# Last stage of a graph network with experts: per-partition layout, a sum on TensorE, and batches of unequal size

## The chip, the cores and the metric

The kernel runs on one core of a Trainium2 chip. A core has five engines that work side by side: TensorE (PE; its weight loads are shown apart as PEld), VectorE (DVE), ScalarE (ACT), GpSimd (POOL) and SyncE (SP), which here issues most of the transfers. Each engine works through its own list of instructions in order and waits on semaphores for the others. Sixteen DMA engines move data between the chip's memory (DRAM) and the on-chip memory SBUF; TensorE writes its results to another memory, PSUM, of eight banks, and each bank holds 512 numbers of four bytes in each partition.

The metric is the time on the device in microseconds (us), the median of several runs. A profile is one further execution, recorded instruction by instruction.

## The reference

Two layers are computed over 6250 nodes of 256 numbers each. The first gathers the 100,000 edges of each node and runs a small network over them. The second, which matters here, sends each node to two of 16 experts:

```
logits  = xn @ gate_w + gate_b                # xn: the normalised node
top 2 experts per node, weights w by softmax of their logits
moe     = sum over the two of  w_k * ((relu(xn @ w1[e_k] + b1[e_k])) @ w2[e_k] + b2[e_k])
y       = xn + moe
out     = x1 + (y - mean(y)) / sqrt(var(y) + 1e-5) * gamma + beta
```

Here x1 is the node after the first layer. All numbers have four bytes.

## The kernel before, in words

Nodes are taken in 50 tiles (NT) of P = 125, one node in each partition. The program has three stages that bear on the change.

**The graph stage** ends by writing x1 to DRAM (x1_d) and by sorting each node, twice, into the rows of its two experts (xg_d).

**The expert stage** works through blocks of 256 sorted rows, at most 57 of them here (NS). For a block, load_block (L996) fetches rows, weights and bias on SP's queue, three blocks ahead. run_block (L1025) multiplies with the first weights in two halves (L1034), and turn_block (L1007) in between transposes the next block: four transposes on TensorE, a copy on VectorE (xT, L1014), the addition of xb and eb (L1017), and two small operations that make the addresses. The first half's activation is ScalarE's (L1040), the second half's is VectorE's (hb, L1038). Then come the second weights (L1047), the addition of the block's input on VectorE (L1050), the scaling by w on ScalarE (L1052), and two scatters from GpSimd (L1053), which put each row back in the order of the nodes: the first choice of node n to row n of y_d, the second to row N + n. The input xn is part of what is scattered, in shares that add up to it, so that y is the sum of the two rows.

**The filling of X** is done during the expert stage. X1 in SBUF holds x1 for all 50 tiles. load_x1 (L979) is called after every third block from block 15 on; it adds beta to the five tiles that the call before has loaded (L984, one VectorE operation of 125x1280) and issues the loads of the next five. Since the order of each engine's list is the order of the program text (manual_schedule), that addition stands on VectorE between L1050 of one block and L1014 for the next one.

**The last stage** (L1353 to L1400) waits for the last scatter. It takes ten batches of five tiles (FS). In each: two loads from y_d, one for each choice, each split in partitions 0 to 79 and 80 to 124 (halves, L100); the addition of the two (L1365); for each tile, statistics in two operations (L1370, L1371); a root on ScalarE (L1372) and a reciprocal and a bias on VectorE (L1377, L1378); the normalisation of each tile on ScalarE (L1382); the product with gamma and the addition of X (L1386, L1387); and the stores. The products of a batch are written between the statistics and the reciprocal of the next one. A node lies in partition p of tile i as row i * 125 + p ("(i p) d -> p i d"), so each partition takes five separate rows of 1 KB from DRAM for a batch. Three batches are loaded ahead, in four pairs of buffers.

Of the kernel before, what the change touches and what calls it, by code (L numbers as in the profile page):

```python
# [9 lines left out]
F32 = mybir.dt.float32  # L10
# [3 lines left out]
AF = mybir.ActivationFunctionType  # L14
OP = mybir.AluOpType
AX = mybir.AxisListType
PSUM = bass.MemoryType.PSUM
DRAM = bass.MemoryType.DRAM

P = 125  # L20
PA = 80
RR = 8
GW = 2
WE = 20
JR = (6, 5, 5, 10, 21, 20, 28)
GR = (1, 1, 1, 2, 3, 2, 1)
JS = 3
KB = 250
GS = 4
FS = 5  # L30
SB = 256
NA = 14
NS = 57
SLOTS = 12
SLOT = 4.6
IB = (1, 1, 1, 2, 3, 5)
# [5 lines left out]
def kernel(  # L42
# [18 lines left out]
    nc = tc.nc  # L61
    N, D = x.shape
    E, EF = edge.shape
# [3 lines left out]
    NT = N // P  # L67
    EJ = E // P
# [12 lines left out]
    NG = (NT + GS - 1) // GS  # L81
    ER = EP * sum(JR)
# [1 line left out]
    REG = [(ER - EP * sum(JR[:c + 1]), j) for c, j in enumerate(JR)]  # L84
    N0 = NT - GS * (NG - 1)
    GRP = [(GS * (NG - 1 - g), GS * (NG - 1 - g) + (GS if g else N0)) for g in range(NG)]
    assert N == NT * P and E == EJ * P and ER % (E // 100) == 0 and NT % FS == 0 and GW + sum(GR) == NG and sum(IB) == NG
    assert NA <= -(-(2 * (N - P * GRP[-2][1]) - NE * (SB - 1)) // SB)
    assert KR == 32 and HC % 4 == 0 and GS * P <= 512 and NT <= GS * NE and wpack.shape[1] == WROW and D == DC * 128 and GF <= 128 and EF <= 128
    assert N0 == 2 and GW == 2 and WE <= RR * JS and P * GRP[GW - 1][0] <= EP * JR[0] <= ER // 2 and all(i == 1 for i in IB[:GW])  # L90
# [5 lines left out]
    x1_d = dram.tile([N, D], F32, name="x1_d")  # L96
    xg_d = dram.tile([NE * N, DR], F32, name="xg_d")
    y_d = dram.tile([2 * N, D], F32, name="y_d")

    def halves(o, i):  # L100

        return [(o[a:z], i[a:z]) for a, z in ((0, PA), (PA, P))]
# [9 lines left out]
    ident = const.tile([128, 128], F32, name="ident")  # L112
# [49 lines left out]
    for c, j in enumerate(JR):  # L162
        k = -(-j // JS)
# [295 lines left out]
    def node_cols(b):  # L459
        g0 = sum(IB[:b])  # L460
        return GRP[g0 + IB[b] - 1][0], GRP[g0][1]
# [36 lines left out]
    def counts(b):  # L498
        a, z = node_cols(b)
        cols = slice(a, z)  # L500
        cnt = ix.tile([P, GS * max(IB)], F32, name="cnt")[:, 0:z - a]
        nc.vector.tensor_sub(cnt, ends[b], rp[:, cols])
        nc.vector.scalar_tensor_tensor(cnt, cnt, nf, cnt_f[:, cols], op0=OP.mult, op1=OP.add)
        nc.vector.tensor_scalar(ne_n[:, cols], cnt, 1.0, None, op0=OP.min)
        nc.vector.tensor_scalar(rc_n[:, cols], cnt, 1.0, None, op0=OP.max)
        nc.vector.reciprocal(rc_n[:, cols], rc_n[:, cols])
        if b < GW:
            nc.vector.tensor_scalar(nw[:, a - W0:z - W0], ne_n[:, cols], nf, None, op0=OP.mult)
# [84 lines left out]
    def mean_window(g, i):  # L593
        t = GRP[g][0] + i
        mean(G[g]["at"][:, i, :], rc_n[:, t:t + 1])
# [274 lines left out]
    MB = {"x1": 0}  # L870
# [107 lines left out]

    def load_x1():  # L979

        t0 = MB["x1"]
        if t0:
            x1 = MB["X1"][:, t0 - FS:t0]
            nc.vector.tensor_tensor(x1, x1, MB["btb"][:, None, :].to_broadcast([P, FS, D]), op=OP.add)  # L984
        if t0 == NT:
            return
        if t0 == 0:
            for t, src in ((MB["gmb"], gamma), (MB["btb"], beta)):
                nc.sync.dma_start(t, bass.AP(tensor=src.tensor, offset=src.offset, ap=[[0, P], [1, D]]))
        for o, i in halves(MB["X1"][:, t0:t0 + FS], x1_d[t0 * P:(t0 + FS) * P].rearrange("(i p) d -> p i d", p=P)):  # L990
            nc.sync.dma_start(o, i)
        MB["x1"] += FS

    BL = [{} for _ in range(NB)]

# [86 lines left out]
    for g, (a, z) in enumerate(GRP):  # L1082
        B, n = SLOTS * g, z - a
# [4 lines left out]
    for g, (a, z) in enumerate(GRP):  # L1088
        B, n = SLOTS * g, z - a
# [59 lines left out]
    for b in range(GW, len(IB)):  # L1149

        a, z = node_cols(b)
# [51 lines left out]
    a, z = GRP[0]  # L1203
# [38 lines left out]
    with tc.If(bad_v != 0):  # L1242

        NC = (KC + 1) * GS * P - 1
        space = chp.tile([P, RR, EF], F32, name="tmp").rearrange("p r f -> p (r f)")
# [4 lines left out]
        for lo in range(0, N, NC):  # L1250
            sums = [wk.tile([128, KC + 1, GS * P], F32, name="inT").rearrange("p k n -> p (k n)")[:EF + 1] for _ in range(2)]
# [17 lines left out]
            for n0 in range(0, min(NC, N - lo), P):  # L1269
                n = min(P, NC - n0, N - lo - n0)  # L1270
# [14 lines left out]
    with tc.manual_schedule():  # L1285
        counts(0)
        for c in range(1, len(JR)):
            load_ids(c)
        for k in range(DC):
            turn(0, k)  # L1290
        for t in reversed(range(a1, z1)):
            find_edge(t)
        bounds(1)
        for i in range(z - a):
            cut = (cut_w, cut_x)[i]
            cut_window_2(0, i, WE // 2, WE, cut)
            cut_window(0, i, 0, WE // 2, cut)
            if i == 0:
                index_windows(1)
                for h in range(2):  # L1300
                    for w in windows_of(rwp.tile([P, RR, JS, 2 * EF], F32, name="rw"), 2):
                        take_window(1, len(G[1].get("win", [])), w)
        for i in range(z - a):
            sum_window_2(0, i, (cut_w, cut_x)[i])
            max_window(0, i)
            mask_window(0, i)
            mean_window(0, i)
        counts(1)
        nc.sync.dma_start(w2s, w2.rearrange("(k p) d -> p k d", p=128))
        for k in range(DC, KC + 1):  # L1310
            turn(0, k)
        cuts += [cut_x, windows_of(rawp.tile([P, RR, JS, EF], F32, name="raw"), 1)[0]]
        keep_x(0)
        load_edges(0)
        stats_x(1, 0)
        stats_x(1, 1)
        at_slot(SLOTS * (GW - 1) - 4, load_edges, 1)

        tasks.sort(key=lambda t: t[:2])
        T, credit = 0, SLOT  # L1320
        clock[0] = 0
        for slot, _, fn, args, cost in tasks:
            while slot > T:
                tell_pe()
                while credit > 0 and T >= SLOTS * (GW - 1) - 3:
                    cost_e = next(stream, None)
                    if cost_e is None:
                        break
                    credit -= cost_e
                g = min(T // SLOTS, NG - 1)  # L1330
                T, credit = T + 1, min(credit, 0.0) + SLOT * (GRP[g][1] - GRP[g][0]) / GS
                clock[0] = T
            if fn is take_edges:
                edges_until(args[0])
            fn(*args)
            credit -= cost
        for b in range(NA, NS):
            run_block(b, NS)
            if b % 3 == 0 and b // 3 - NA // 3 - 1 <= NT // FS:
                load_x1()  # L1340
    with tc.If(nc.values_load(MB["more"][0:1, 0:1]) != 0):
        with tc.manual_schedule():
# [7 lines left out]
    X1, gmb, btb = MB["X1"], MB["gmb"], MB["btb"]  # L1350


    with tc.tile_pool(name="yl", bufs=4) as yl, tc.tile_pool(name="ft", bufs=3) as ft, \  # L1353
            tc.tile_pool(name="fm", bufs=FS + 2) as fm, tc.manual_schedule():
        ys, outs, sums = {}, {}, {}

        def load_y(t0):
            ys[t0] = [yl.tile([P, FS, D], F32, name="yk%d" % k) for k in range(2)]
            for k in range(2):
                for o, i in halves(ys[t0][k], y_d[k * N + t0 * P:k * N + (t0 + FS) * P].rearrange("(i p) d -> p i d", p=P)):  # L1360
                    nc.sync.dma_start(o, i)

        def add_y(t0):
            y = ys[t0][0]
            nc.vector.tensor_add(y, y, ys[t0][1])  # L1365
            mv = fm.tile([P, FS, 2], F32, name="mvc")
            rs, nb = (fm.tile([P, FS], F32, name=nm) for nm in ("rsc", "nbc"))
            for i in range(FS):
                bs = fm.tile([P, 6], F32, name="bsc")
                nc.vector.bn_stats(bs, y[:, i, :])  # L1370
                nc.vector.bn_aggr(mv[:, i, :], bs)  # L1371
            nc.scalar.activation(rs, mv[:, :, 1], AF.Sqrt, bias=eps_t)  # L1372
            sums[t0] = mv, rs, nb

        def norm_y(t0):
            mv, rs, nb = sums.pop(t0)
            nc.vector.reciprocal(rs, rs)  # L1377
            nc.vector.scalar_tensor_tensor(nb, mv[:, :, 0], -1.0, rs, op0=OP.mult, op1=OP.mult)  # L1378
            y = ys.pop(t0)[0]
            outs[t0] = o = ft.tile([P, FS, D], F32, name="o")  # L1380
            for i in range(FS):
                nc.scalar.activation(o[:, i, :], y[:, i, :], AF.Identity, scale=rs[:, i:i + 1], bias=nb[:, i:i + 1])  # L1382

        def write_out(t0):
            o = outs.pop(t0)
            nc.vector.tensor_tensor(o, o, gmb[:, None, :].to_broadcast([P, FS, D]), op=OP.mult)  # L1386
            nc.vector.tensor_add(o, o, X1[:, t0:t0 + FS, :])  # L1387
            for o_, i_ in halves(out[t0 * P:(t0 + FS) * P].rearrange("(i p) d -> p i d", p=P), o):
                nc.sync.dma_start(o_, i_)

        for t0 in range(0, 3 * FS, FS):
            load_y(t0)
        for t0 in range(0, NT, FS):
            add_y(t0)
            if t0:
                write_out(t0 - FS)
            if t0 + 3 * FS < NT:
                load_y(t0 + 3 * FS)
            norm_y(t0)
        write_out(NT - FS)  # L1400


# [35 lines left out]
```

## Time and profile before

| | us |
|---|---|
| median of 3 runs (lowest, highest) | 1454.03 (1452.14, 1459.58) |
| profiled execution, its own time | 1462.48 |
| its span, first to last instruction | 1460.7 |
| PE busy in the span | 1148.5 (79%) |
| DVE busy | 915.6 (63%) |
| ACT busy | 511.0 (35%) |
| POOL busy | 527.8 (36%) |

The span is what the profile's times count from. The profile's clock is the share of TensorE's full speed that was granted; over the span it was 0.900. A busy share of an engine is a mean over stages with different limits: the expert stage and the last stage look nothing alike.

In lists of groups a line names the line of the kernel, engine, operation, what is written and read, the shapes and the count; then the busy time in us and the mean duration of one in ns; then how long the engine had been idle just before these instructions and what ended the wait. In tables of stretches a row gives the stretch, its length, each engine's busy time with the number of instructions, the clock, the mean busy share of the DMA engines, and GB/s. In the timeline and the chain of waits a row starts with the start and the duration.

### The profile page before, as it was taken

Reading aid. Unit: us, or ns where it says so; the run is one execution under the profiler, and the core shown is the slowest. Engines: PE = TensorE matmul, PEld = TensorE weight load, DVE = VectorE, ACT = ScalarE, POOL = GpSimd, SP = SyncE. Lnnn points to the kernel's source line nnn. Section 1 sums busy time; section 2 is a strip of 40 time slices with the busy share of each in tenths; the row PEclk is TensorE's granted clock in tenths of the full one; section 3 lists DMA queues with packets and bytes.
Section 4 is the critical chain, followed back from the end, with each engine's and each line's share of the span. In section 5 each row is a group of like instructions: output and inputs, shape, how many; then the busy total and the mean of one; then the engine's idle time right before and its main releaser. Section 6 shows DMA issues by size and latency. Waiting matters only on the chain.

```text
span 1460.7 us, 16116 instructions
## 1 busy us (share of the span) xinstructions
PE 1148.5 (79%) x4667; PEld 810.4 (55%) x4667; DVE 915.6 (63%) x2322; ACT 511.0 (35%) x1174; POOL 527.8 (36%) x611
## 2 busy tenths in 40 slices
PE   2857258978786879999688999899999999999200
PEld 1743144635443445655445567787888888888100
DVE  4487569959685979988688323244344544444397
ACT  3384125543445542542325441321212222212133
POOL 4133033563546553364242522234333333333100
PEclk9988579989988889999899999899999999999655
DMA  6726777787778897888887332646777787765695
GB/s 180 168 63 172 187 193 201 194 224 182 216 192 247 223 277 190 254 223 213 249 221 206 84 122 69 209 147 235 229 250 262 234 267 234 237 226 184 128 263 148
DMA packets 173812, 292.25 MB, mean 200 GB/s; under 512 B 30883, under 2 KB 119656, under 8 KB 166414
## 3 DMA queue, kind: packets, MB, share of 16 engines
q1 hardware_dynamic: 137374, 234.35, 56.0%
q0 software_dynamic: 36224, 56.33, 13.7%
q8 instruction: 40, 0.66, 0.2%
q14 instruction: 62, 0.51, 0.1%
q10 hardware_dynamic: 112, 0.41, 0.1%
HBM read 169.70 MB, written 123.21 MB: 201 GB/s over the span
## 4 chain that ended last, share of the span: by engine, by line
issue 27%; DVE 23%; DMA 18%; POOL 13%; PE 12%; ACT 3%; SPq 2%; POOLq 0%; DVEq 0%; ACTq 0%
POOL y_d L1053 9%; PE acc L747 5%; DMA raw<-in_edge_dram 5%; DMA cg<-carry_d,next_i 4%; DMA rows_d<-rw 3%; PE acc L755 3%; DVE rw L302 2%; DVE rw L299 2%; DVE rw L298 2%; DMA xg_d<-xr,pos_i 2%; DVE rw L301 2%; POOL gb L474 1%; PE acc L570 1%; DMA carry_d<-ct 1%; DVE o L1387 1%
## 5 line engine op out<-in xcount | busy, mean ns | idle before, releaser
L747 PE MATMUL acc<-inT,w1x 128*128 128x500 f32 (+1 forms) x832 | 375.9, 603 | 0.0
L747 PEld LDWEIGHTS acc<-inT,w1x 128*128 128x128 f32 x832 | 163.1, 204 | 179.1 <-issue 177.3
L1053 POOL DMA_INDIRECT y_d<-yb,to_i x114 | 134.5, 1180 | 295.6 <-ACT yb L1052 273.4
L1034 PE MATMUL acc<-xT,wt 128*128 128x256 f32 x912 | 225.6, 391 | 7.8 <-ACT hb L1040 6.2
L1047 PE MATMUL acc<-wt,hb 128*128 128x256 f32 x912 | 209.6, 383 | 3.6 <-DVE hb L1038 3.6
L860 POOL DMA_INDIRECT xg_d<-xr,pos_i x100 | 130.1, 1301 | 213.8 <-DVE xr L856 152.2
L755 PE MATMUL acc<-w2s,hT 128*125 128x256 f32 x800 | 193.5, 400 | 13.4 <-ACT hT L749 13.4
L1034 PEld LDWEIGHTS acc<-xT,wt 128*128 128x128 f32 x912 | 171.0, 193 | 40.2 <-ACT hb L1040 14.9
L1047 PEld LDWEIGHTS acc<-wt,hb 128*128 128x128 f32 x912 | 175.3, 192 | 29.0 <-DVE hb L1038 4.5
L755 PEld LDWEIGHTS acc<-w2s,hT 128*125 128x125 f32 x800 | 157.8, 201 | 39.5 <-ACT hT L749 14.2
L1052 ACT ACTIVATE yb<-yb,xb 128x256 f32<-128x256 f32 x114 | 51.8, 501 | 349.0 <-issue 291.6
L1050 DVE TENSOR_TENSOR yb<-acc,xb 128x512 f32<-128x512 f32 x57 | 39.4, 692 | 167.3 <-PE acc L1047 167.3
L749 ACT ACTIVATE hT<-acc,c 128x500 f32<-128x500 f32 (+1 forms) x104 | 68.5, 658 | 209.0 <-PE acc L747 209.0
L474 POOL DMA_INDIRECT gb<-in_dst_dram,blk_i x50 | 71.1, 1421 | 130.5 <-DVE blk_i L471 73.8
L301 DVE TENSOR_TENSOR rw<-rw,raw 125x768 f32<-125x768 f32 x88 | 83.6, 950 | 32.7 <-DMA raw<-in_edge_dram 32.7
L298 DVE TENSOR_TENSOR rw<-rw,keep 125x768 f32<-125x768 f32 x81 | 78.3, 966 | 34.0 <-DMA rows_d<-rw 23.7
L1014 DVE COPY xT<-pT 128x512 f32<-128x512 f32 x57 | 39.4, 690 | 72.4 <-PE pT L1012 71.5
L302 DVE TENSOR_TENSOR rw<-rw,raw 125x768 f32<-125x768 f32 x88 | 83.6, 950 | 0.0
L299 DVE TENSOR_TENSOR rw<-rw,bar 125x768 f32<-125x768 f32 x81 | 79.4, 981 | 0.0
L705 POOL DMA_INDIRECT cg<-carry_d,next_i x44 | 65.1, 1481 | 36.8 <-issue 23.6
L698 POOL DMA_INDIRECT at<-rows_d,first_i x44 | 60.0, 1363 | 37.2 <-PE acc L747 10.0
L732 ACT COPY inT<-pT 128x500 f32<-128x500 f32 (+1 forms) x65 | 36.0, 553 | 98.8 <-PE pT L731 94.8
(296 smaller groups left out, 1445.1 us busy)
## 6 DMA issues: line engine op xcount, KB each, us to landing
wt<-in_wpack_dram SPq DMA_DIRECT2D x57, 1026.0 KB
rows_d<-rw SPq DMA_DIRECT2D x27, 1440.0 KB
rows_d<-rw SPq DMA_DIRECT2D x27, 810.0 KB
raw<-in_edge_dram SPq DMA_DIRECT2D x27, 720.0 KB
xb<-xg_d SPq DMA_DIRECT2D x57, 258.0 KB
raw<-in_edge_dram SPq DMA_DIRECT2D x27, 405.0 KB
yk<-y_d SPq DMA_DIRECT2D x20, 400.0 KB
eb<-in_eb_dram SPq DMA_DIRECT2D x57, 128.0 KB
```

The costliest lines, as they stand in the source:

```text
L298: nc.vector.tensor_tensor(su, prev[0], keep[c][:, :, s + j, None].to_broadcast(bcast), op=OP.mult)
L299: nc.vector.tensor_tensor(mx, prev[1], bar[c][:, :, s + j, None].to_broadcast(bcast), op=OP.min)
L301: nc.vector.tensor_tensor(su, su, x_j, op=OP.add)
L302: nc.vector.tensor_tensor(mx, mx, x_j, op=OP.max)
L474: nc.gpsimd.indirect_dma_start(out=gbs_[t], out_offset=None, in_=dst_b, in_offset=IndirectOffsetOnAxis(ap=blk_i[:, t:t + 1], axis=0))
L747: nc.tensor.matmul(pH[:, :n * P], w1x[:, k, ms], inT[:, k, :n * P], start=False, stop=(k == KC - 1))
L749: nc.scalar.activation(h[:, :n * P], pH[:, :n * P], AF.Relu, bias=c1[:, m:m + 1])
L755: nc.tensor.matmul(pO, G[g]["hT"][m][:, i * P:(i + 1) * P], w2s[:, m, :], start=(m == 0), stop=(m == HC - 1))
L860: d = nc.gpsimd.indirect_dma_start(out=xg_d[:, :], out_offset=IndirectOffsetOnAxis(ap=G[g]["pos"][:, i, k:k + 1], axis=0), in_=G[g]["xr"][ ...
L1034: nc.tensor.matmul(pB[i][:, half, :], wt[:, k * FF + m * 128:k * FF + (m + 1) * 128], xT[:, k, :], start=(k == 0), stop=(k == DC - 1))
L1047: nc.tensor.matmul(pY[:, h, :], hb[:, m, h * 128:(h + 1) * 128], wt[:, W2O + m * D:W2O + (m + 1) * D], start=(m == order[0]), stop=(m == o ...
L1053: d = nc.gpsimd.indirect_dma_start(out=y_d[:, :], out_offset=IndirectOffsetOnAxis(ap=BL[b]["to"][:, h:h + 1], axis=0), in_=yb[:, h, :], in ...
```

## The change

1. **Layout.** Within a batch of n tiles, a node's place is now row p * n + i: partition p takes n rows that follow each other in DRAM. The same holds for X, y and the output (of_batch).
2. **Batches.** Fourteen batches of 1, 2, 2, 3, 4, six times 5, 4, 2 and 2 tiles take the place of ten of five. Four are loaded ahead, in five pairs of buffers.
3. **Sum.** The two loads of a tile are added by two matmuls with the identity that accumulate in PSUM; two tiles share a bank, and all eight banks are used. Statistics and normalisation read PSUM. The sums of batch k + 1 are written after the statistics of batch k.
4. **X.** load_x1 handles two batches at a call: it adds beta in two operations, one after the other, and issues the loads of the next two. It is called after every fourth block from block 16 on.
5. **Order.** In an iteration, the loads are now issued before the stores.

```diff
-FS = 5
+BT = (1, 2, 2, 3, 4) + 6 * (5,) + (4, 2, 2)
...
+    BATCH = [(sum(BT[:k]), sum(BT[:k + 1])) for k in range(len(BT))]
+
+    def of_batch(t, k):
+        a, z = BATCH[k]
+        return t[a * P:z * P].rearrange("(p i) d -> p i d", p=P)
...
     def load_x1():
-        t0 = MB["x1"]
-        if t0:
-            x1 = MB["X1"][:, t0 - FS:t0]
-            nc.vector.tensor_tensor(x1, x1, MB["btb"][:, None, :].to_broadcast([P, FS, D]), op=OP.add)
-        if t0 == NT:
-            return
-        if t0 == 0:
+        k0 = MB["x1"]
+        for a, z in BATCH[max(k0 - 2, 0):k0]:
+            x1 = MB["X1"][:, a:z]
+            nc.vector.tensor_tensor(x1, x1, MB["btb"][:, None, :].to_broadcast([P, z - a, D]), op=OP.add)
+        if k0 == 0:
...
-        for o, i in halves(MB["X1"][:, t0:t0 + FS], x1_d[t0 * P:(t0 + FS) * P].rearrange("(i p) d -> p i d", p=P)):
-            nc.sync.dma_start(o, i)
-        MB["x1"] += FS
+        for k in range(len(BATCH))[k0:k0 + 2]:
+            for o, i in halves(MB["X1"][:, BATCH[k][0]:BATCH[k][1]], of_batch(x1_d, k)):
+                nc.sync.dma_start(o, i)
+            MB["x1"] += 1
...
             run_block(b, NS)
-            if b % 3 == 0 and b // 3 - NA // 3 - 1 <= NT // FS:
+            if b % 4 == 0 and b // 4 - NA // 4 - 1 <= len(BATCH) // 2:
                 load_x1()
...
-    with tc.tile_pool(name="yl", bufs=4) as yl, tc.tile_pool(name="ft", bufs=3) as ft, \
-            tc.tile_pool(name="fm", bufs=FS + 2) as fm, tc.manual_schedule():
+    with tc.tile_pool(name="yl", bufs=5) as yl, tc.tile_pool(name="ft", bufs=3) as ft, \
+            tc.tile_pool(name="py", bufs=8, space=PSUM) as py, \
+            tc.tile_pool(name="fm", bufs=max(BT) + 2) as fm, tc.manual_schedule():
...
-        def add_y(t0):
-            y = ys[t0][0]
-            nc.vector.tensor_add(y, y, ys[t0][1])
...
+        def add_y(k):
+            ps = []
+            for i in range(BT[k]):
+                if i % 2 == 0:
+                    bank = py.tile([P, 2, D], F32, name="py")
+                ps.append(bank[:, i % 2, :])
+                for c in range(2):
+                    nc.tensor.matmul(ps[i], ident[:P, :P], ys[k][c][:, i, :], start=(c == 0), stop=(c == 1))
...
+        def stats_y(k):
...
+                nc.vector.bn_stats(bs, ps[i])
...
-        for t0 in range(0, 3 * FS, FS):
-            load_y(t0)
-        for t0 in range(0, NT, FS):
-            add_y(t0)
-            if t0:
-                write_out(t0 - FS)
-            if t0 + 3 * FS < NT:
-                load_y(t0 + 3 * FS)
-            norm_y(t0)
-        write_out(NT - FS)
+        NK = len(BT)
+        for k in range(4):
+            load_y(k)
+        add_y(0)
+        for k in range(NK):
+            stats_y(k)
+            if k + 1 < NK:
+                add_y(k + 1)
+            if k + 4 < NK:
+                load_y(k + 4)
+            if k:
+                write_out(k - 1)
+            norm_y(k)
+        write_out(NK - 1)
```

More of the change, by code (lines that the diff above doesn't have):

```diff
@@ L86 @@
     GRP = [(GS * (NG - 1 - g), GS * (NG - 1 - g) + (GS if g else N0)) for g in range(NG)]
-    assert N == NT * P and E == EJ * P and ER % (E // 100) == 0 and NT % FS == 0 and GW + sum(GR) == NG and sum(IB) == NG
+    assert N == NT * P and E == EJ * P and ER % (E // 100) == 0 and sum(BT) == NT and GW + sum(GR) == NG and sum(IB) == NG
+    assert len(BT) % 2 == 0 and (NS - 1) // 4 - NA // 4 - 1 >= len(BT) // 2 and NA % 4
     assert NA <= -(-(2 * (N - P * GRP[-2][1]) - NE * (SB - 1)) // SB)
@@ L1350, with load_y @@
     X1, gmb, btb = MB["X1"], MB["gmb"], MB["btb"]
-    with tc.tile_pool(name="yl", bufs=4) as yl, tc.tile_pool(name="ft", bufs=3) as ft, \
-            tc.tile_pool(name="fm", bufs=FS + 2) as fm, tc.manual_schedule():
+    with tc.tile_pool(name="yl", bufs=5) as yl, tc.tile_pool(name="ft", bufs=3) as ft, \
+            tc.tile_pool(name="py", bufs=8, space=PSUM) as py, \
+            tc.tile_pool(name="fm", bufs=max(BT) + 2) as fm, tc.manual_schedule():
         ys, outs, sums = {}, {}, {}
[L1357 to L1361, printed above, removed]
-        def add_y(t0):
-            y = ys[t0][0]
[L1365 to L1368, printed above, removed]
+        def load_y(k):
+            n = BT[k]
+            ys[k] = [yl.tile([P, max(BT), D], F32, name="yk%d" % c)[:, 0:n] for c in range(2)]
+            for c in range(2):
+                for o, i in halves(ys[k][c], of_batch(y_d[c * N:(c + 1) * N, :], k)):
+                    nc.sync.dma_start(o, i)
+        def add_y(k):
[4 more added lines that the diff above has]
+                ps.append(bank[:, i % 2, :])
+                for c in range(2):
+                    nc.tensor.matmul(ps[i], ident[:P, :P], ys[k][c][:, i, :], start=(c == 0), stop=(c == 1))
+            ys.pop(k)
+            sums[k] = ps
+        def stats_y(k):
+            n, ps = BT[k], sums[k]
+            mv = fm.tile([P, max(BT), 2], F32, name="mvc")[:, 0:n]
+            rs, nb = (fm.tile([P, max(BT)], F32, name=nm)[:, 0:n] for nm in ("rsc", "nbc"))
+            for i in range(n):
@@ L1369, in add_y, with norm_y @@
                 bs = fm.tile([P, 6], F32, name="bsc")
-                nc.vector.bn_stats(bs, y[:, i, :])
+                nc.vector.bn_stats(bs, ps[i])
                 nc.vector.bn_aggr(mv[:, i, :], bs)
             nc.scalar.activation(rs, mv[:, :, 1], AF.Sqrt, bias=eps_t)
-            sums[t0] = mv, rs, nb
-        def norm_y(t0):
-            mv, rs, nb = sums.pop(t0)
+            sums[k] = ps, mv, rs, nb
+        def norm_y(k):
+            ps, mv, rs, nb = sums.pop(k)
             nc.vector.reciprocal(rs, rs)
@@ L1378, in norm_y @@
             nc.vector.scalar_tensor_tensor(nb, mv[:, :, 0], -1.0, rs, op0=OP.mult, op1=OP.mult)
[L1379 to L1388, printed above, removed]
-                nc.sync.dma_start(o_, i_)
@@ L1391 @@
-        for t0 in range(0, 3 * FS, FS):
-            load_y(t0)
-        for t0 in range(0, NT, FS):
-            add_y(t0)
-            if t0:
-                write_out(t0 - FS)
-            if t0 + 3 * FS < NT:
-                load_y(t0 + 3 * FS)
-            norm_y(t0)
-        write_out(NT - FS)
+            outs[k] = o = ft.tile([P, max(BT), D], F32, name="o")[:, 0:BT[k]]
+            for i in range(BT[k]):
+                nc.scalar.activation(o[:, i, :], ps[i], AF.Identity, scale=rs[:, i:i + 1], bias=nb[:, i:i + 1])
@@ new lines, in write_out @@
+        def write_out(k):
+            o, n = outs.pop(k), BT[k]
+            nc.vector.tensor_tensor(o, o, gmb[:, None, :].to_broadcast([P, n, D]), op=OP.mult)
+            nc.vector.tensor_add(o, o, X1[:, BATCH[k][0]:BATCH[k][1], :])
+            for o_, i_ in halves(of_batch(out, k), o):
+                nc.sync.dma_start(o_, i_)
+        NK = len(BT)
[11 more added lines that the diff above has]
+            norm_y(k)
```

## The prediction

> **What bounds the kernel now.** I read the chain of waits first, around the start of the last stage.
>
> ```profile
> 1354.95 12.22 DMA y_d<-yb,to_i
> ...
> 1367.31 0.34 SPq L1361
> ...
> 1370.63 11.05 DMA yk<-y_d
> ...
> 1381.81 1.50 DVE yk L1365
> ```
>
> The columns are start, length, who. The last scatter lands at 1367.17, the first load is issued at 1367.31, and from there to 1460.70 the stage has 93.4 us to itself. Three batches are loaded together and share the queue, so VectorE starts only at 1375.90 (timeline) and is on the chain from 1381.81 to its last instruction. The groups of that stretch say what it does:
>
> ```profile
> L1370 DVE BATCH_NORM_STATS2 bsc<-yk 125x6 f32<-125x256 f32 x50 | 20.1, 401 | 0.3
> L1365 DVE TENSOR_TENSOR yk<-yk,yk 125x1280 f32<-125x1280 f32 x10 | 14.9, 1493 | 16.5 <-DMA yk<-y_d 16.4
> L1387 DVE TENSOR_TENSOR o<-o,X 125x1280 f32<-125x1280 f32 x10 | 14.9, 1492 | 0.3
> L1386 DVE TENSOR_TENSOR o<-o,gmb 125x1280 f32<-125x1280 f32 x10 | 14.8, 1482 | 2.7 <-ACT o L1382 2.7
> ```
>
> In the timeline one batch starts at 1404.29 and the next at 1411.83: 7.54 us, of which the add of the two results is 1.53, statistics 2.68, the two output operations 3.02, reciprocal and bias 0.31. DMA is the runner-up (columns: length, PE, PEld, DVE, ACT, POOL busy, clock, DMA share, GB/s):
>
> ```profile
> 1376.00:1389.00 13.00, 0.00 (x0) 0.00 (x0) 11.29 (x27) 3.17 (x7) 0.00 (x0) 0.50 1.11 217
> 1389.00:1434.00 45.00, 0.00 (x0) 0.00 (x0) 43.29 (x90) 17.20 (x36) 0.00 (x0) 0.50 1.05 264
> ```
>
> VectorE is 96% busy and the DMA engines are full too: 217 GB/s while only loads run, 264 with stores among them. TensorE is idle at half clock.
>
> The change also touches the expert phase, where TensorE is busy without a break. One block of it with a load_x1 call, and the line of an ordinary block for comparison:
>
> ```profile
> 1088.97 0.69 DVE L1014 COPY xT<-pT 128x512 f32<-128x512 f32 x1 [1.47 <-PE pT L1012]
> ...
> 1094.99 1.48 DVE L984 TENSOR_TENSOR X<-X,btb 125x1280 f32<-125x1280 f32 x1
> ...
> 1096.55 0.69 DVE L1014 COPY xT<-pT 128x512 f32<-128x512 f32 x1
> ...
> 1098.12 0.94 DVE L1038 TENSOR_SCALAR hb<-acc,wt 128x256 f32<-128x256 f32 x2
> 1098.31 3.62 PE L1047 MATMUL acc<-wt,hb 128*128 128x256 f32 x16
> ```
>
> The addition of beta to X fills exactly the 1.47 us in which VectorE otherwise waits for the transposes: today it costs nothing.
>
> [...] in this stretch TensorE waited 1.53 us for an activation and kept clock 1.00:
>
> ```profile
> 912.00:915.50 3.50, 2.02 (x12) 1.56 (x10) 1.96 (x4) 2.85 (x6) 1.84 (x3) 1.00 0.68 181
> ```
>
> [...] (copy of 512 from PSUM 690 ns, add of 512 from SBUF 680)[...] (256 from PSUM at L1040 458 ns, from SBUF at L1382 589). [...]
>
> **The change part by part.**
>
> *Sum moved to TensorE.* It removes 10 x 1.53 = 15.3 us of VectorE. It adds, per tile, two matmuls of 256 columns; the trace shows two instructions per written one (912 at L1034 for 57 x 8 written), and 16 at L1047 take 1098.31 to 1101.77, 0.216 each. So 4 x 0.216 = 0.86 us a tile at full clock, 1.73 at half; 4.3 or 8.6 us a batch of five. The cover is VectorE's 6.0 us a batch: hidden at full clock, bare at half. The pause then is 1.7 us a batch, near the 1.53 that kept the clock. Eight banks hold 16 tiles, so TensorE works one to two batches ahead[...]. Its waits queue only further sums behind them; the new wait of the statistics for the sums has the output operations of the batch before behind it on VectorE, and for those the stores on SP. Statistics now read PSUM: [...] I take 0.5, the measured neighbour. ScalarE's normalisation gets faster and is covered by the next statistics in full batches; I leave 0.6 for six near ties.
>
> *Fourteen batches for ten.* Statistics 0.53 a tile and 2 x 0.267 a tile for output (1.49 us for 1280 elements, 0.16 fixed) are 1.07 a tile, 53.2 us; the rest of 6.01 is 0.69 a batch, x 14 = 9.7. VectorE's work: 62.9 (before: 75.4).
>
> *Small batch first.* Four loads at 0.44 us each (chain) end at 1369.1; some 2 us to land (by estimate, from the last stores: issued by 1456.1, 2.4 us of transfer for 640 KB at 264 GB/s, end at 1460.7, leaves 2.2), 1.7 us of sums at half clock, and statistics start at 1373.1 instead of 1375.9. Then the next loads, four issues each, and the cold sums keep VectorE waiting 1.8 us before batch 1; the root on ScalarE, with nothing to cover it, 0.4.
>
> *Small batches last.* With 5, 4, 2, 2 tiles ScalarE's normalisation isn't covered by shorter statistics: waits of 0.3, 0.95, 0 and 1.25, together 2.5 (before: 2.7, once). The last store is 256 KB, 1.0 us of transfer instead of 2.4: end 4.1 after VectorE instead of 5.5.
>
> So VectorE: 62.9 + 2.2 + 2.5 + 0.5 + 0.6 = 68.7 against 79.3 (1375.9 to 1455.2), 10.6 less; start 2.8 earlier; store 1.4 less. Stage: -14.8.
>
> *Side by side in memory.* Packets grow from 1 KB to up to 5 KB; 150 x 128 KB = 19.2 MB must move in some 73 us, 263 GB/s, which the old packets nearly made. Larger ones are therefore worth nothing on the sum if DMA is hidden; their bound below is the old 217/264, which I work out as a rival. SP issues 84 DMAs for 60 (24 x 0.44 = 10.6 us), but outside the first batches it is waiting for VectorE's output anyway; a load queues behind the store two batches back and still has three batches (18 us) to land. Batch 4 needs no free buffer, with five.
>
> *X in pairs of batches, every fourth block.* Seven groups of loads, 28 DMAs for 20, are issued behind load_block; the next weights queue behind at most 1.28 MB (4-5 us), with three blocks (22.7 us) of lead. But the additions come two in a row. Pairs of (4,5), (5,5), (5,5), (5,4) tiles take 2.7 or 3.0 us where 1.47 is covered, so the xT copy and all behind it on VectorE move by 1.25 or 1.53. Behind it stands hb (L1038), which TensorE needs: the first of its two is done at 1098.60, and its matmul, third of four, is due at 1098.31 + 4 x 0.216 = 1099.17; the weights load goes 0.2 ahead, slack 0.4. Stalls: 2 x 0.85 + 2 x 1.1 = +3.9 us, nothing absorbs them since TensorE has no idle time there. Bounds: 0 if slack is larger than I read, 5.6 if there is none. The small pairs (1.1 to 1.65 us) fit.
>
> Sum: -14.8 + 3.9 = -10.9. Against the profiled execution (span 1460.7, its time 1462.5) that is a span of 1449.8; against the median 1454.03 it is **1443.1**, as the profiled execution was one of the longer ones and the difference lies in a stage that any execution has.
>
> **Rivals.** *TensorE stays at half clock* (slower): place, the sums; price 50 x 1.73 = 86.4 us from 1371.2, then some 5 us of last batch and 4.1 of store: stage end 1466.7, plus 3.9, is +9.9: 1464. For it: the stage starts cold and the pause is 1.7 us a batch. Against: a cold TensorE here is busy without a break[...]. At share f of cold time a tile costs 0.864/(1 - f/2); TensorE becomes the bound above f = 0.57, and the kernel slower than before above 0.86.
>
> *Larger packets give nothing or less.* At 217 and then 264 GB/s the last load lands near 1438, when VectorE wants it at 1437: 1 to 2 us lost. If the rate stays near 220 throughout, 19.2 MB need 87 us from 1368.2: stage end about 1457.5, total near 1455, no change. For it: full DMA engines at 217. Against: that rate goes with 1 KB packets.
>
> *Expert stalls larger* (5.6, or the next block's transposes late too): 1445 to 1448.
>
> *No stall and a warm start* (faster): -3.9 and -1.5: 1438.
>
> **How the numbers follow.** The likeliest case 0.66, half clock 0.10, slow DMA 0.14, larger stalls or other losses 0.10; the warm, stall-free variant lies inside the first. The range 1438 to 1453 runs from that variant to the milder part of slow DMA[...] and stalls at 5.6 (+1.7); it leaves out half clock and the worst of DMA. Half a per cent, 7.3 us, is about what can be told from no change. Faster by more: 0.60 + 0.05 of DMA + 0.06 of stalls = 0.71; within: 0.06 + 0.06 + 0.04 = 0.16; slower: 0.10 + 0.03 = 0.13.
>
> **What would show it.** First statistics 5.8 us (not 8.6) after the first load; full batches every 6.0 to 6.1 us with VectorE over 90% busy; clock 1.00 from some 10 us into the stage; statistics at 0.40 to 0.41 us from PSUM; last store 4.1 us after VectorE; and in four expert blocks a gap of about 1 us before L1047, released by hb. It is wrong if sums release VectorE in full batches at a clock of 0.5, if loads do, or if these gaps are missing.

## The result

| | us |
|---|---|
| the changed kernel, median of 19 runs (lowest, highest) | 1451.62 (1444.57, 1469.03) |
| the kernel before, median of 19 runs (lowest, highest) | 1459.45 (1452.14, 1467.06) |
| ratio, 95% interval | 0.995 (0.9932 to 0.9968) |
| span of the profiled execution (before: 1460.7) | 1442.8 |

The change is worth 0.5%, some 7.3 us, where 10.9 were forecast; 1451.6 lies inside the range. The spans of the two profiled executions differ by more, 17.9 us, but most of the surplus lies ahead of the change: stages that are the same in both end earlier or later from one execution to the next. The last stage's first load is issued at 1359.76 here, at 1367.31 before, and between 1358.6 and 1374.3 in the runs below. So I read two lengths that leave this out. From the first load to the end of the span, the **last stage** takes 83.0 us (93.4 before). From L1050's addition (here L1057) of block 14 to that of block 56, the **expert stage** takes 321.1 us (318.4 before). Together: -10.4 + 2.8 = -7.6, close to the 7.8 between the medians.

The groups of the last stage after the change; before, VectorE's L1365 and its 16.5 us of waiting stood here:

```profile
L1380 PE MATMUL py<-yk,ident 125*125 125x256 f32 x200 | 49.8, 402 | 20.4 <-DMA yk<-y_d 20.0 <-ACT o L1401 0.4
L1401 ACT ACTIVATE o<-py,nbc,rsc 125x256 f32<-125x256 f32 x50 | 24.3, 563 | 40.2 <-DMA out_dram<-o 17.2 <-DVE nbc L1398 13.5 <-issue 5.9
L1390 DVE BATCH_NORM_STATS2 bsc<-py 125x6 f32<-125x256 f32 x50 | 20.4, 407 | 14.0 <-PE py L1380 14.0
```

The sums are TensorE's, and statistics from PSUM cost 407 ns (401 before, from SBUF). New is ScalarE's 17.2 us in front of the normalisation, which the view puts down to stores. Part of that it would have waited anyway, for the bias of the batch (L1398); counted from the end of that bias in the trace, the first normalisation starts 9.3 us late in all batches together, 4.9 us of it in batch 3 (0.7 in all in the kernel before). The stage in three stretches:

```profile
1359.80:1369.00 9.20, 6.50 (x14) 4.22 (x15) 1.28 (x5) 2.14 (x3) 0.00 (x0) 0.51 0.65 199
1369.00:1419.00 50.00, 39.99 (x174) 31.35 (x173) 41.75 (x115) 18.85 (x44) 0.00 (x0) 1.00 0.99 287
1419.00:1443.00 24.00, 3.27 (x15) 2.22 (x13) 16.93 (x38) 7.95 (x19) 0.00 (x0) 0.66 0.43 127
```

TensorE has its full clock from 1369 to 1419 (1.00, after 0.51). In the middle, VectorE is busy for 41.75 of 50 us (43.29 of 45 before), and the DMA engines are full at 287 GB/s, share 0.99 (264, share 1.05). What VectorE waits for (us in total, times, longest), and one of these waits in the timeline:

```profile
DVE bsc L1390 <- PE py L1380: 14.0, 4, 11.5
DVE o L1405 <- ACT o L1401: 7.4, 7, 3.1
DVE rsc L1397 <- ACT rsc L1392: 1.8, 1, 1.8
DVE o L1405 <- DMA out_dram<-o: 0.3, 1, 0.3
```

```profile
1372.77 1.15 SPq L1408 DMA_DIRECT2D out_dram<-o  x2
...
1381.78 1.47 ACT L1401 ACTIVATE o<-py,nbc,rsc 125x256 f32<-125x256 f32 x3 [6.17 <-DMA out_dram<-o]
...
1383.28 0.96 DVE L1405 TENSOR_TENSOR o<-o,gmb 125x768 f32<-125x768 f32 x1 [3.09 <-ACT o L1401]
```

The store of batch 0, a single tile, is issued from 1372.77; only at 1381.78 may ScalarE write to the buffer it came from, which it needs for batch 3, since there are three of them (ft). By 1372.77 the loads of 17 tiles, 4.35 MB, had been issued ahead of that store; in the trace the last seven of them, 1.98 MB, had not yet landed. VectorE stands still for 3.09 us. Stores are also issued late: VectorE had finished batch 1 at 1373.38 (two tiles, L1406), but SP issues its store from 1380.10 on, behind the four loads of batch 6, and only after a load issued at 1370.76, eight issues earlier, had landed.

One of the two expert blocks in which two additions of five tiles stand in a row (block 33):

```profile
1168.61 2.88 DVE L992 TENSOR_TENSOR X<-X,btb 125x1280 f32<-125x1280 f32 x2
...
1171.41 0.68 DVE L1021 COPY xT<-pT 128x512 f32<-128x512 f32 x1
...
1172.98 0.88 DVE L1045 TENSOR_SCALAR hb<-acc,wt 128x256 f32<-128x256 f32 x2
1173.52 0.70 PE L1054 MATMUL acc<-wt,hb 128*128 128x256 f32 x2 [0.56 <-DVE hb L1045]
```

TensorE now waits for hb, 0.56 us here. Four blocks take 8.14, 8.41, 8.41 and 8.14 us, all others from 14 on 7.58.

### The profile page after: what moved, and what is told of

The parts are those of the page before. It is cut to its first block, busy times and chain, and to the rows that moved or that the text cites. A ratio compares the mean times of both kernels' runs of the same rounds, so it can differ in the third digit from the quotient of the medians.

```text
span 1442.8 us, 16610 instructions
## 1 busy us (share of the span) xinstructions
PE 1191.0 (83%) x4867; PEld 843.2 (58%) x4867; DVE 900.1 (62%) x2332; ACT 510.5 (35%) x1178; POOL 527.2 (37%) x611
## 5 line engine op out<-in xcount | busy, mean ns | idle before, releaser
L755 PE MATMUL acc<-inT,w1x 128*128 128x500 f32 (+1 forms) x832 | 371.5, 598 | 0.0
L1041 PE MATMUL acc<-xT,wt 128*128 128x256 f32 x912 | 221.2, 385 | 7.8 <-ACT hb L1047 6.2
L763 PE MATMUL acc<-w2s,hT 128*125 128x256 f32 x800 | 197.4, 406 | 16.5 <-ACT hT L757 16.5
L1041 PEld LDWEIGHTS acc<-xT,wt 128*128 128x128 f32 x912 | 168.1, 190 | 39.2 <-ACT hb L1047 16.9
L1057 DVE TENSOR_TENSOR yb<-acc,xb 128x512 f32<-128x512 f32 x57 | 39.4, 691 | 164.7 <-PE acc L1054 164.7
L706 POOL DMA_INDIRECT at<-rows_d,first_i x44 | 62.4, 1418 | 36.5 <-issue 15.7
```

The costliest lines, as they stand in the source:

```text
L755: nc.tensor.matmul(pH[:, :n * P], w1x[:, k, ms], inT[:, k, :n * P], start=False, stop=(k == KC - 1))
L763: nc.tensor.matmul(pO, G[g]["hT"][m][:, i * P:(i + 1) * P], w2s[:, m, :], start=(m == 0), stop=(m == HC - 1))
L1041: nc.tensor.matmul(pB[i][:, half, :], wt[:, k * FF + m * 128:k * FF + (m + 1) * 128], xT[:, k, :], start=(k == 0), stop=(k == DC - 1))
```

## The experiments

Each is the changed kernel with one edit. The last stage's length is read from the profile as above. Of the changed kernel itself I have two readings, 83.0 and 85.2, so a difference of one or two microseconds between single profiles says little. All lengths first; a dash was not tried:

| last stage, us | three output buffers | six output buffers |
|---|---|---|
| as changed | 83.0, 85.2 | 79.0, 80.8; 80.9 with X split |
| sum on VectorE | 91.6 | 88.9 |
| packets of 1 KB | 87.2 | 81.0 |
| batches of five | 85.4 | 81.7 |
| half of the loads left out | 73.9 | - |
| stores issued by ScalarE | 91.8 | - |

**Six output buffers.**

```diff
-        tc.tile_pool(name="ft", bufs=3) as ft
+        tc.tile_pool(name="ft", bufs=6) as ft
```

> Six output buffers (o) in place of three, all else as in the changed kernel, whose last stage took 83.0 us from the first load to the end. Theory O (a store queues behind loads, and with three buffers ScalarE waits for it): ScalarE's waits for stores, 17.2 us, go to under 2; the stage takes 78 to 79.5 us. Theory D (the DMA engines' rate is the bound, the buffers only show it): the waits move to the loads (statistics for sums, sums for loads, over 3 us in all) and the stage takes 81.5 us or more.

79.0 us. ScalarE no longer waits for a store, and these are VectorE's waits:

```profile
DVE bsc L1390 <- PE py L1380: 15.5, 7, 11.5
DVE o L1405 <- ACT o L1401: 2.1, 2, 1.1
DVE rsc L1397 <- ACT rsc L1392: 1.8, 1, 1.8
DVE o L1405 <- DMA out_dram<-o: 0.4, 1, 0.4
```

The 7.4 us behind ScalarE became 2.1, of which the tail's 1.1 and 1.0 remain; 1.5 us came back as waits for sums, that is for loads. By this reading theory O holds and D contributes.

> Six output buffers once more, to see how far 79.0 us repeat: 79 to 81 us for the last stage, blocks 14 to 56 in 321.1 us, no wait of over 1 us for a store; ratio to the kernel before about 0.992.

80.8 us, above O's range and below D's; ratio 0.9931 (0.9906 to 0.9956). There is again no wait of ScalarE for a store, but VectorE's waits for sums after the first are 5.9 us (2.5 with three buffers). So O and D both have a part. The interval overlaps that of the changed kernel (0.9932 to 0.9968): the gain of the buffers, 2.1 to 6.2 us from reading to reading, rests on the lengths of the stage, in which six buffers are shorter in each of the four pairs of the table, and not on the medians.

**Half of the loads.** The second choice is left out, and the first is added twice.

```diff
-            ys[k] = [yl.tile([P, max(BT), D], F32, name="yk%d" % c)[:, 0:n] for c in range(2)]
-            for c in range(2):
+            ys[k] = [yl.tile([P, max(BT), D], F32, name="yk0")[:, 0:n]] * 2
+            for c in range(1):
```

> Leaves out the loads of the second choice; TensorE adds the first one twice, so 12.8 MB move in the last stage and not 19.2. Every instruction of TensorE, VectorE and ScalarE stays. Theories O and D alike: stores no longer wait long, the stage falls from 83.0 to 76 to 79 us. Rival C (the sums, the cold clock or ScalarE's rows lose the time, transfers only show at the side): 81 us or more.

73.9 us, lower than either theory said, with three output buffers:

```profile
DVE bsc L1390 <- PE py L1380: 12.4, 2, 11.5
DVE o L1405 <- ACT o L1401: 2.4, 3, 1.1
DVE rsc L1397 <- ACT rsc L1392: 0.4, 1, 0.4
```

No wait for a store is left (17.2 us in the changed kernel) although the buffers are three: it is the loads that made stores late. SP now waits 41.9 us for VectorE's output and never for a load. Rival C falls as far as TensorE, VectorE and ScalarE go, which carry out the same instructions; SP issues 28 loads fewer. One of ScalarE's instructions stands elsewhere, however: the table load on the line of its root (ACT_TABLE_LOAD, 1.28 us) ran before the statistics here, as in the kernel before, but after them in the changed kernel, so that VectorE waited 1.8 us for that root and here 0.4. Without these 1.4 us the gap to the 79 to 81 us with six buffers is 3.7 to 5.6 us; so much the loads of the second choice, their issues included, cost the stage where no store is waited for.

**Stores from ScalarE's queue.**

```diff
-                nc.sync.dma_start(o_, i_)
+                nc.scalar.dma_start(o_, i_)
```

> The stores of the last stage are issued from ScalarE's queue, three output buffers as in the changed kernel. Theory O: a queue of their own lets stores pass the loads that were issued before them; ScalarE's waits for stores fall from 17.2 to under 5 us, the stage takes 78 to 80 us (83.0 now). Theory D: the same bytes in the same engines, 82 us or more, and loads come later in their place.

91.8 us: not theory O, and 10 us above the 82 from which theory D's open range began. The timeline of ScalarE shows one reason:

```profile
1378.44 0.81 ACTq L1408 DMA_DIRECT2D out_dram<-o  x2
1379.35 1.48 ACT L1401 ACTIVATE o<-py,nbc,rsc 125x256 f32<-125x256 f32 x3 [2.17 <-DVE nbc L1398]
```

A pair of issues takes ScalarE 0.81 us here, right ahead of the next normalisation, which is the one operation that the batch waits for. The loads did not run on freely either: in the trace SP issues one at 1385.97 and the next at 1394.85, when a store issued by ScalarE at 1386.22 had landed, and the statistics waited longer for sums (eleven waits instead of four). ScalarE's waits for stores did fall, to 4.8 us in one place, but the edit changed two other things, so it does not settle its question.

**Old layout.**

```diff
-        return t[a * P:z * P].rearrange("(p i) d -> p i d", p=P)
+        return t[a * P:z * P].rearrange("(i p) d -> p i d", p=P)
```

> A node lies at row i * 125 + p of its batch again (packets of 1 KB), all else as in the changed kernel. If larger packets carry bytes faster (257 to 290 GB/s in the changed kernel, 253 to 267 before): the stage takes 86 to 91 us and GB/s fall to 265 or less. If packets' size is worth nothing here: 82 to 84 us.

87.2 us, 2 to 4 more. The waits show where:

```profile
ACT o L1401 <- DMA out_dram<-o: 24.5, 5, 7.5
...
DVE o L1405 <- ACT o L1401: 10.5, 7, 3.9
```

More waiting for stores, then, 24.5 us against 17.2. Over 50 us, from 9 us into the stage on, the DMA engines carried 257 GB/s, against 287 and 271 in the two executions of the changed kernel, so both parts of the first expectation came true. With six output buffers:

> Six output buffers and 1 KB packets (rows i * 125 + p). If larger packets are worth their rate whatever the buffers: 82.5 to 85.5 us against 79.0 to 80.9. If they only shortened the queue in front of the stores: 81 us or less, since nothing waits for stores any more.

81.0 us, within the scatter of the 79.0 to 80.9 with large packets, at the value that the rival named. VectorE's waits for sums from twelve microseconds into the stage on are 4.4 us, and 2.4 to 4.5 with large packets, though the rate is lower here too (265 GB/s against 278 to 288). A gain of a microsecond is possible but not shown. As far as single profiles tell, most of what the layout gives to this kernel, it gives by shortening the queue in front of the stores.

**Sum on VectorE.**

```diff
-                for c in range(2):
-                    nc.tensor.matmul(ps[i], ident[:P, :P], ys[k][c][:, i, :], start=(c == 0), stop=(c == 1))
+            y = ys[k][0]
+            nc.vector.tensor_add(y, y, ys[k][1])
...
```

The call moves to the head of its own batch, and statistics and normalisation read SBUF again.

> The sum of the two results back on VectorE (one addition a batch, ahead of the statistics, which read SBUF again); layout, batches, X and buffers as in the changed kernel. If VectorE's work still sets the stage: 50 x 0.267 + 14 x 0.19 = 16 us more work, of which 5 us go into the waits for stores that are there anyway: 92 to 96 us for the stage (83.0 now). If transfers set it: under 88 us.

91.6 us, just below the range: of all the changes to the last stage together, 8.2 to 10.4 us, 1.8 remain without this one. With six output buffers:

> The sum on VectorE and six output buffers. If the sum's 16 us of VectorE work are hidden in part by waits for stores: nothing is left to hide in and the stage takes 90 to 92 us, so that moving the sum is worth 10 to 12 us with six buffers (79.0, 80.9) against 6 to 8.5 with three (83.0, 85.2 against 91.6). Rival (six buffers help this one by 4 us too): 87 to 88.5 us.

88.9 us, between the two. Moving the sum takes 16 us of work off VectorE, and the stage gains 6.4 to 8.6 us of it with three output buffers and 8.0 to 9.9 with six; the remainder becomes waiting for transfers.

**Batches of five.**

```diff
-BT = (1, 2, 2, 3, 4) + 6 * (5,) + (4, 2, 2)
+BT = 10 * (5,)
```

X is then filled in five pairs of five, and blocks 14 to 56 take 324.2 us; the length of the last stage leaves that out.

> Ten batches of five again (X in pairs of five), with the sum on TensorE and rows side by side. Theory (small first batches start early but use up three output buffers while the loads ahead of their stores fill the queue): ScalarE's waits for stores fall from 17.2 to under 8 us, the tail costs 4 to 6 us more, the stage takes 83 to 87 us, so that unequal batches are worth 0 to 4 us. Rival (small batches are worth the 8 to 9 us that the forecast gave to start, tail and store less four more batches' fixed cost): 88 us or more.

85.4 us: ScalarE's waits for stores are 7.0 us, as the theory had it, and unequal batches are worth 0.2 to 2.4 us. The end after VectorE's last operation is only 1.7 us longer (5.4 against 3.7); the tail was expected to cost 4 to 6. With six output buffers:

> Ten batches of five with six output buffers (85.4 us with three; unequal batches take 83.0 to 85.2 with three and 79.0 to 80.9 with six). Theory (three buffers cost the unequal batches 4 us because the early stores of small batches queue behind loads, and cost batches of five less): 83.5 to 85.5 us, so that unequal batches are worth 3 to 6 us once buffers suffice. Rival (more buffers help any batches alike): 80 to 82 us.

81.7 us, in the rival's range: unequal batches are worth 0.8 to 2.7 us, and the larger gain that I expected once buffers suffice isn't there. Small batches start the stage early (first statistics 4.6 us after the first load, against 11.2 and 11.0 with batches of five), but what they win there goes again later: VectorE works 60.0 us in fourteen batches and 57.6 in ten, and with three output buffers 74.8 us pass between its first and last instruction where batches of five take 68.7; most of the rest is waits (12.0 us for 8.5). The shortage of output buffers is not theirs alone: batches of five gained 3.7 us from more of them.

**Six output buffers and X split.** The second of the two additions is moved behind the next block.

```diff
-        for a, z in BATCH[max(k0 - 2, 0):k0]:
-            x1 = MB["X1"][:, a:z]
-            nc.vector.tensor_tensor(x1, x1, ...)
+        add_beta(k0 - 2)
...
+            if b % 4 == 1 and 0 < b // 4 - NA // 4 - 1 <= len(BATCH) // 2:
+                add_beta(2 * (b // 4 - NA // 4 - 1) - 1)
```

> Six output buffers, and of the two additions of beta that load_x1 makes in a row the second is moved behind the next block. Theory (two separate losses): the four expert blocks of 8.14 and 8.41 us go back to 7.58, blocks 14 to 56 take 318.3 us in place of 321.1; the last stage takes 79.0 us as with six buffers alone. Against the kernel before the span is 14.3 us shorter, ratio near 0.990. Rival (the stall only moves to the next block): 321 us again.

Median 1444.56 us, ratio 0.9904 (0.9875 to 0.9933); blocks 14 to 56 take 318.4 us, every one 7.58, and the last stage 80.9. One of the blocks that had stalled, with each addition in the gap of its own:

```profile
1169.66 1.48 DVE L992 TENSOR_TENSOR X<-X,btb 125x1280 f32<-125x1280 f32 x1
1171.22 0.69 DVE L1026 COPY xT<-pT 128x512 f32<-128x512 f32 x1
...
1177.24 1.48 DVE L992 TENSOR_TENSOR X<-X,btb 125x1280 f32<-125x1280 f32 x1
1178.80 0.69 DVE L1026 COPY xT<-pT 128x512 f32<-128x512 f32 x1
```

So the two losses are separate, and both can be had back. This version has the lowest median and ratio of all that were timed over several runs. Beside it, in the same comparison, the changed kernel:

> The changed kernel itself, to see how far its last stage repeats: 83.0 us within 1, blocks 14 to 56 in 321.1 us, ratio to the kernel before 0.995.

Ratio 0.9938 (0.9918 to 0.9958); blocks 14 to 56 in 321.1 us; but 85.2 us for the last stage, outside the microsecond that I gave it. The intervals of the two ratios overlap a little, but the times themselves hardly do: five of the six of the version with both repairs (median 1444.56) lie below the lowest of the changed kernel's eleven (1448.42, median 1451.00).

## Why the prediction was right or wrong

**TensorE and its clock: right.** That the clock would rise within the first 10 us of the stage was my estimate. Measured: the sums start at 1362.17, the mean clock is 0.51 up to 1369, 9 us into the stage, and 1.00 from there to 1419; the rival of half clock did not happen. In the second execution of the changed kernel one stretch of 10 us shows a mean clock of 0.83 (so does 1383 to 1393 in the second with six output buffers); by my estimate from that mean, 3.4 us of it were at clock 0.50. The sums took no work of VectorE's, and statistics from PSUM cost 6 ns more (407 against 401), within the 10 ns that the prediction took from a copy of 512 from PSUM (690 ns) and an addition of 512 from SBUF (680). For ScalarE the prediction compared two different operations (458 and 589 ns); the same one, the normalisation, takes 563 ns from PSUM and 589 from SBUF.

**Start and end: right, the gains forecast a little too small.** First statistics came 4.5 us after the first load (5.8 forecast), the end 3.7 us after VectorE (4.1). The 8.6 set beside the 5.8 is where VectorE's addition started before; the first statistics came 10.1 us after the first load then.

**X in pairs: mechanism right, size two fifths too large.** Four blocks stalled at the place and by the wait that were named, 2.8 us for 3.9. The slack of 0.4 us was right; the term that was too large is the shift of xT, since two additions in a row take 2.88 us, not 3.0, and xT moved by 1.25 us (3.41 us after L1057 instead of 2.16), not 1.53.

**The step that failed: stores at no cost.** In "side by side in memory" the prediction let SP's 84 DMAs go because SP waits for VectorE's output anyway, and priced a late load; in "small batches last" it counted the last store. Nowhere did it ask who waits for the other stores. That is ScalarE, through three output buffers, and VectorE behind it. Nor did SP wait for VectorE. Its own waits, before and after:

```profile
SPq L1389 <- DVE o L1387: 43.5, 10, 6.6
SPq L1361 <- DMA yk<-y_d: 2.9, 7, 0.7
```

```profile
SPq L1408 <- DVE o L1406: 17.2, 5, 5.0
SPq L1370 <- DMA yk<-y_d: 12.9, 17, 1.5
SPq L1408 <- DMA yk<-y_d: 11.4, 13, 1.5
```

All of the 17.2 us fall after 1418, when the last load has been issued; until then SP issued loads and stores as earlier transfers landed.

From its first to its last instruction VectorE took 74.8 us (1364.30 to 1439.07) where 68.7 were summed. The forecast held 5.3 us of waits (2.2 + 2.5 + 0.6), the list after the first statistics holds 12.0 (2.5 + 7.4 + 1.8 + 0.3). Of the 6.7 us between them, 4.6 are waits behind ScalarE and the stores (7.7 for 2.5 + 0.6). With six buffers the stage takes 79.0 to 80.9 (mean 80.2), against the 78.6 that the sum gave (93.4 - 14.8) and a mean of 84.1 with three: that one wait accounts for most of the error, some 3.9 of 5.5 us by these means.

**A smaller term: the first root, 0.4 us forecast, 1.8 measured.** ScalarE's table load, which stands on the root's line, ran before the stage in the kernel before, and after the first statistics in the changed one:

```profile
1361.46 1.28 ACT L1372 ACT_TABLE_LOAD   x1
```

```profile
1365.09 1.28 ACT L1392 ACT_TABLE_LOAD   x1 [11.28 <-DVE mvc L1391]
```

That is 1.4 us of the 6.7; the other 0.7 are waits for sums (2.5 for 1.8). Why the table load stands there now, no run tells.

**The rival on DMA: right on the resource, wrong on the path.** It expected the last loads to come late, 1 to 2 us. The DMA engines were indeed full (share 0.99 at 287 GB/s), but loads made stores late first. That larger packets are worth nothing "if DMA is hidden" stood on the same oversight: with three buffers they are worth 2 to 4 us, most of it by way of the stores, as far as single profiles tell.

**The difference against the medians.** -14.8 + 3.9 was forecast; -10.4 + 2.8 was measured in the first profile, -8.2 + 2.8 in the second. The absolute 1443.1 was also tied to a median of three runs that lay 5.4 us below that of nineteen.

What stays open: how much of the remaining 3.7 to 5.6 us between six buffers and half of the loads belongs to the rate of the transfers and how much to their order; how much of the stores' lateness comes from part 5 of the change, which put the loads of an iteration ahead of its stores and was undone in no run; and the exact value of unequal batches, which is near the scatter of a single profile.

## What to carry to other kernels

When an engine is relieved, follow every buffer of its stage around the whole ring, the output buffers too: here a store issued behind 1.98 MB of loads under way held its buffer for 9.0 us, and the small batches came back to it soonest. Ask of the issuing engine, too, what its next issue waits for. Work that fits exactly into a wait is free only once: one addition of 1.48 us in a wait of 1.47 left the expert blocks at 7.58 us here, and two in a row (2.88 us) made them 8.41, so that the second cost 0.8 us of its 1.4. Where the stages ahead vary by more than the change, compare lengths of stages in the profiles beside the medians.

## What the runs showed of the hardware

A one-tile store, issued while 1.98 MB of loads ahead of it were under way, released its buffer 9.0 us later (1372.77 to 1381.78). Full DMA engines (share 0.99) carried 287 GB/s in the middle of this stage with packets of up to 5 KB, 271 in a second execution, and 257 in the same kernel with packets of 1 KB: 1.05 to 1.12 times as much with the larger ones. ScalarE took 0.81 us to issue two stores (1378.44, stores from its queue) and started no normalisation meanwhile. A table load of ScalarE took 1.28 us; where it ran after the first statistics, VectorE waited 1.8 us for the root, and 0.4 where it had run before. And two VectorE additions of 1280 elements in a row took 2.88 us, not twice 1.48, as the second began before the first had ended (1170.01 and 1170.09 in block 33).
